# Five PSUM banks in one pool, a turned tile in the warming bank, and logits turned in 32x32 squares, in a two-layer graph attention kernel

## The chip, the cores and the metric

The kernel runs on one core of one Trainium2 chip. The time is device microseconds of one execution. The core has five engines with queues of their own: TensorE (PE in the profile; its weight loads, which overlap its products, are shown apart as PEld), VectorE (DVE), ScalarE (ACT), GpSimd (POOL) and SyncE (SP). TensorE writes its results to PSUM, a memory of eight banks, each 128 partitions by 512 f32 columns; VectorE and ScalarE empty the banks into SBUF. An engine carries out its queue in order and waits on semaphores that other engines or DMAs raise.

## The reference

512 nodes with 768 features each, 8704 edges (a random graph made symmetric, and a loop at each node). Two layers of graph attention, then a residual and a layer norm:

```
def gat_layer(x, W, a_s, a_d, b, edge_index, concat):
    h = (x @ W).reshape(n, H, C)
    alpha_s = einsum('nhc,hc->nh', h, a_s);  alpha_d = einsum('nhc,hc->nh', h, a_d)
    e = leaky_relu(alpha_s[src] + alpha_d[dst], 0.2)
    m = segment_max(e, dst);  e = exp(e - m[dst])
    alpha = e / (segment_sum(e, dst)[dst] + 1e-16)
    return segment_sum(h[src] * alpha[:, :, None], dst) + b

h   = elu(gat_layer(x, W1, a_src1, a_dst1, b1, ...))   # 8 heads of 768: W1 is 768 x 6144
out = gat_layer(h, W2, a_src2, a_dst2, b2, ...)        # 1 head: W2 is 6144 x 768
x   = layernorm(x + out)
```

## The kernel before

The edges become a dense 512x512 matrix of counts, made on the chip from the sorted edge list by products of one-hot matrices, so that each attention is a dense masked softmax and each sum over edges a matrix product. All products are f32; the profile shows an f32 product as two records. Large products use block schemes with fewer multiplications: seven products P1 to P7 of half-size blocks, or fifteen of thirds, with sums of blocks formed by VectorE or by DMAs that add. Several products add up in the same PSUM bank (`over`).

The order on each engine is that of the Python code (`manual_schedule`). It runs: load and turn x; head 0's projection x @ W1 between the counting of edges; then for each head the projection of a later head, the attention's logits and softmax, the attention product, elu, and the head's share of the second layer's projection, added up in `h2`; at last the second layer's logits, softmax and product, and the layer norm. Code for a second, general pass follows, which is entered only if the list of edges is not of the expected kind; it isn't for these inputs.

Three places are touched.

**Pools.** A tile pool in PSUM is a set of banks; a new tile takes a free bank, and its first writer waits until the bank's former tile has been read for the last time. Before, up to the end of head 0's counting stage there are `mm0` with three banks and `held` with two, the latter for product P1 of the first projection, whose bank is used again by P6, P7 and P4 (L659 to L692). Beside them stand `tr` with two banks and `bc` with one. At the end of the counting stage (`counting.close()`) `mm0` and `held` are given back, and a pool `mm` of five banks over the same space is opened for the rest.

**Turning x.** `turn_x(t, r)` (L323) turns three 128x128 squares of x by TensorE into a tile of PSUM (L327), and ScalarE copies it to `xT` (L328). After the third item of the first projection, four tiles are turned: (2, 0), (3, 0), (2, 1), (3, 1). VectorE then forms the sums `xS` (L425 to L428), of which product P5 needs the first. The pool `bc` at that time is used by nothing: at the kernel's start, products of zeros were written to it to keep TensorE's clock up (L292), which is why it is called the warming bank here. Later in the counting stage one tile of counts goes there.

**Layer 2's logits.** TensorE adds up both logits of each node in a tile `rows`, as two rows at each of the partitions 0, 32, 64 and 96 (L1535): source logits on the first, destination logits on the second. ScalarE copies it to `row2` (L1564). Then `pick`, called inside the second tile of product P7 ahead of its last piece, sums the four partial rows: one product spreads the source logits over all partitions as `BC` (L1570), and four products, one for each tile of 128 nodes, turn the destination logits into a column each of `own` (L1572):

```
nc.tensor.matmul(BC[H][:, :N], picks[:, 0:1].to_broadcast([P, P]), row2, start=True, stop=True)
for t in range(NT):
    nc.tensor.matmul(own[:, t:t + 1], row2[:, t * P:(t + 1) * P], picks[:, 1:2], start=True, stop=True)
```

VectorE copies `own` to `own2` (L1575), ScalarE adds it to `BC` tile by tile (`lift`, L723), VectorE applies the slope (L727) and takes the maximum (L732), ScalarE the exponential (L736). VectorE meanwhile subtracts or adds the products' banks to `h2` (L570) and folds a common part into it (L1530, `fold(parts[:2])` between `row2` and `pick`). Product P4 of the second layer adds to P7's banks and so waits until L570 has read them.

Other lines that the text names: L389 turns the edge indices; L383 casts them on VectorE; L445 is the product of halves; L483 to L485 empty head 1's products P1, P2 and P6; L585 sums weights on VectorE; L672 empties head 0's products on VectorE; L706 spreads logits by TensorE; L712 is a VectorE transposition of 128x32; L1033 turns the attention by DMA and L1036 puts it into `PT`; L1072 to L1075 form sums of it; L1139 and L1145 are head 0's attention products and their emptying; L1626 is the last product; L274 and L275 are sums of weights by DMA.

Of the kernel before, what the change touches and what calls it, by code (L numbers as in the profile page):

```python
# [8 lines left out]
F32 = mybir.dt.float32  # L9
# [5 lines left out]
ALU = mybir.AluOpType  # L15
AX = mybir.AxisListType
# [23 lines left out]
def gat_pass(  # L40
# [16 lines left out]
    nc = tc.nc  # L57
    P = 128
    N, D = x.shape
    H = a_src1.shape[0]  # L60
    E = src.shape[0]
    NT = N // P
# [6 lines left out]
    SQ = 32  # L69
# [4 lines left out]
    const = ctx.enter_context(tc.tile_pool(name="const", bufs=1))  # L74
# [7 lines left out]
    counting = ExitStack()  # L82
    ohp = counting.enter_context(tc.tile_pool(name="onehot", bufs=1))
    tr = ctx.enter_context(tc.tile_pool(name="tr", bufs=2, space=bass.MemoryType.PSUM))
    bc = ctx.enter_context(tc.tile_pool(name="bc", bufs=1, space=bass.MemoryType.PSUM))
    mm = counting.enter_context(tc.tile_pool(name="mm0", bufs=3, space=bass.MemoryType.PSUM))
    held = counting.enter_context(tc.tile_pool(name="held", bufs=2, space=bass.MemoryType.PSUM))

    def row_bcast(ap_row):
        return bass.AP(tensor=ap_row.tensor, offset=ap_row.offset, ap=[[0, P], [1, D]])  # L90
# [209 lines left out]
    ident = const.tile([P, P], F32, name="ident")  # L300
# [5 lines left out]
    ones = const.tile([P, 1], F32, name="ones")  # L306
    nc.vector.memset(ones, 1.0)

    picks = const.tile([P, 2], F32, name="picks")
    for j in range(2):  # L310
        nc.vector.tensor_reduce(picks[:, j:j + 1], ident.rearrange("p (j k) -> p k j", k=32)[:, j, :], axis=AX.X,
                                op=ALU.add)
    far = const.tile([P, 1], F32, name="far")
    nc.vector.memset(far, -NO_EDGE)
    tiny = const.tile([P, 1], F32, name="tiny")
# [4 lines left out]
    xT = keep.tile([P, DC, N], F32, name="xT")  # L320


    def turn_x(t, r):  # L323

        ps = mm.tile([P, 512], F32, name="mm")
        for k in range(HK):
            nc.tensor.transpose(ps[:, k * P:(k + 1) * P], x_sb[:, t, (r * HK + k) * P:(r * HK + k + 1) * P], ident)  # L327
        nc.scalar.copy(xT[:, r * HK:(r + 1) * HK, t * P:(t + 1) * P],  # L328
                       ps[:, :HALF].rearrange("p (k n) -> p k n", n=P))
# [13 lines left out]
    else:  # L343
# [5 lines left out]
        for c in range(EC):  # L349
            m = (c + 0.5) * P * N / E  # L350
            b = int(m // B)
# [96 lines left out]
    HS, AL, BC = {}, {}, {}  # L448
# [22 lines left out]
    def by_halves(hs, XA, B_, p4_apart=False):  # L471
# [19 lines left out]
        if p4_apart:  # L491
# [10 lines left out]
                 P1=("z", (0, 1), -1.0), P10=("y", (1, 1), -1.0), P5=("z", (1, 1), 1.0), P14=("x", (0, 1), -1.0),  # L502
# [149 lines left out]
    def first_projection(h, XA, B_, between):  # L652


        HS[h] = hs = hpool.tile([P, NT, D], F32, name="hs")
        new_alpha(h)
        bank = {}

        def step(p, over, i, out, op):  # L659
            def multiply():  # L660
                if over is None:
                    bank[p, i] = (held if p == "P1" else mm).tile([P, 512], F32, name="held" if p == "P1" else "mm")
                else:
                    bank[p, i] = bank[over, i]
                product(bank[p, i], XA, B_, p, i, over is None)

            def empty():
                ps, o = bank[p, i][:, :HALF], out(i)
                if op is None:
                    nc.scalar.copy(o, ps)  # L670
                else:
                    nc.vector.tensor_tensor(o, o, ps, op=op)  # L672
            return multiply, empty, op is not None

        steps = [
            ("P1", None, lambda i: hs[:, i, L], None),
            ("P2", None, lambda i: hs[:, i, L], ALU.add),
            ("P5", None, lambda i: hs[:, 2 + i, R], None),
            ("P3", "P5", lambda i: hs[:, i, R], None),
            ("P6", "P1", lambda i: hs[:, i, R], ALU.subtract),  # L680
            ("P7", "P1", lambda i: hs[:, 2 + i, R], ALU.subtract),
            ("P4", "P1", lambda i: hs[:, 2 + i, L], None),
        ]

        def firsts():
            for k in range(HK):
                if k == HK - 1:
                    between()
                for i in range(2):
                    if k == 0:  # L690
                        bank["P1", i] = held.tile([P, 512], F32, name="held")
                    nc.tensor.matmul(bank["P1", i][:, :HALF], XA["P1"][:, k, i * P:(i + 1) * P], B_["P1"][:, k, :],  # L692
                                     start=k == 0, stop=k == HK - 1, skip_group_check=True)

        items = [step(p, over, i, out, op) for p, over, out, op in steps for i in range(2)]
        for i, multiply in enumerate((firsts, lambda: None)):
            items[i] = (multiply, *items[i][1:])
        return items
# [66 lines left out]
    if not general:  # L765
# [76 lines left out]
                    done.add(t)  # L842


        turns = {3: [(2, 0), (3, 0), (2, 1), (3, 1)]}
        sums = const.tile([P, 2 * NT + 2], F32, name="sums")
        wholes = len(items)

# [13 lines left out]
        pos, made, quarter, waiting, masks = 0, set(), EC // NT, [], []  # L862
        for n, batch in enumerate(batches):
            fresh = sorted({c // quarter for c in batch} - made)
            made.update(fresh)
            if n == 0:
                waiting = [lambda k=k: destinations(k) for k in fresh]
            else:
                first = ahead_of.get(n, [])
                head = 1 if n == 1 else len(waiting)  # L870
                here = None
                if n + 1 == len(batches):
                    (k,), (before, *rest) = fresh, waiting
# [12 lines left out]
            ahead = kinds(batches[n + 1], True) if n + 1 < len(batches) else []  # L886
            items_here = max(wants[n] - pos if n < len(wants) else 0, 1)
            share = len(ahead) // (items_here + 1) if n == 0 else -(-len(ahead) // items_here)
            for f in masks:
                f()  # L890
            waiting, masks = [], []
            for f in extra.pop(n, []):
                f()
            while n < len(wants) and pos < wants[n]:
                if pos == wholes:
                    pairs = projection(1, XA, B1)
                    items += [(m, e, False) for m, e in pairs[:4]]
                multiply, empty, on_vector = items[pos]
                multiply()
                if on_vector:  # L900
                    waiting.append(empty)
                else:
                    empty()
                pos += 1
                for t, r in turns.get(pos, []):
                    turn_x(t, r)
                if pos == 1:
                    nc.scalar.activation(nidx, low, AF.Copy, bias=0.5)
                part = 0 if n == 0 and pos == 2 else share
                for c in ahead[:part]:  # L910
                    one_hot(c, True)
                del ahead[:part]
            for c in ahead:
                one_hot(c, True)
            if n == 2:
                turn_b1()
            if n == 0:
                ((k,),) = [sorted({c // quarter for c in batches[1]} - made)]
                made.add(k)
                destinations(k)  # L920
                waiting.pop()()
            uncounted += batch
            if n + 1 == len(batches):
                for t in range(NT):
                    half(t, 0)()
            if n == 2 or n + 1 == len(batches):
                count(uncounted, n > 2)
                uncounted = []
# [25 lines left out]
    else:  # L954
        for t in range(NT):
            ps = mm.tile([P, 512], F32, name="mm")
# [29 lines left out]
    counting.close()  # L986


    mm = ctx.enter_context(tc.tile_pool(name="mm", bufs=5, space=bass.MemoryType.PSUM))
    late = ctx.enter_context(tc.tile_pool(name="late", bufs=1))  # L990
    h2 = late.tile([P, NT, D], F32, name="h2")
    pass_ = late.tile([P, 2, 2 * TH], F32, name="pass")
# [7 lines left out]
    work = ctx.enter_context(tc.tile_pool(name="work", bufs=2))  # L1000
# [527 lines left out]
    def fold(parts):  # L1528
        for part, i, op in parts:
            nc.vector.tensor_tensor(part, part, u2[:, i, :], op=op)  # L1530
# [31 lines left out]
        add_rows(al2[:, :, t], ident, t, slice(t * P, (t + 1) * P), False, True)  # L1562
    row2 = work.tile([P, N], F32, name="nr")
    nc.scalar.copy(row2, rows[:, :N])  # L1564
    fold(parts[:2])
    own = tr.tile([P, 512], F32, name="tr")

    def pick():
        BC[H] = bc.tile([P, 512], F32, name="bc")
        nc.tensor.matmul(BC[H][:, :N], picks[:, 0:1].to_broadcast([P, P]), row2, start=True, stop=True)  # L1570
        for t in range(NT):
            nc.tensor.matmul(own[:, t:t + 1], row2[:, t * P:(t + 1) * P], picks[:, 1:2], start=True, stop=True)  # L1572

    pairs[7][0](pick)
    nc.vector.tensor_copy(own2, own[:, :NT])  # L1575
# [105 lines left out]
```

## Time and profile before

| | us |
|---|---|
| median of 3 executions | 615.52 (614.91 to 615.61) |
| profiled execution, its own time | 615.07 |
| its span from first to last instruction | 613.0 |
| TensorE (PE) busy | 604.9 (99%) |
| weight loads (PEld) busy | 481.9 (79%) |
| VectorE (DVE) busy | 525.3 (86%) |
| ScalarE (ACT) busy | 335.4 (55%) |
| GpSimd (POOL) busy | 145.5 (24%) |

The granted TensorE clock is 0.998 of full speed. Busy time of TensorE includes the pipeline's modelled ends, so rows of products overlap by a few hundredths to tenths of a microsecond; a row's start is the firmer number. "Idle before" is the time for which an engine stood still ahead of a row, with the instruction or DMA that ended it; idle time of an engine that nobody waits for costs nothing.

### The profile page before, as it was taken

The numbers are of one execution on the slowest core, as the hardware profiler recorded it, in microseconds if no ns is written. First come the engines' busy times: TensorE is split into PE (matmuls) and PEld (weight loads), VectorE is DVE, ScalarE is ACT, GpSimd is POOL, SyncE is SP. The second block draws the span as 40 slices with busy tenths as digits, with TensorE's granted clock in tenths as the row PEclk, the third lists the DMA queues.
The fourth block names the chain that finished last, engine by engine and source line by source line (L and its number), as shares of the span: only waits on it lengthen the run. The fifth ranks groups of instructions, "written<-read, shape, count | busy, mean of one in ns | idle before, by whom it ended". The sixth has DMA issues, their size and how long they took to land.

```text
span 613.0 us, 8592 instructions
## 1 busy us (share of the span) xinstructions
PE 604.9 (99%) x2772; PEld 481.9 (79%) x2772; DVE 525.3 (86%) x1149; ACT 335.4 (55%) x628; POOL 145.5 (24%) x182
## 2 busy tenths in 40 slices
PE   9999999999999999999999999999999999999995
PEld 5665775558888888888888888888888888885553
DVE  7999889887999879977898879977898878978785
ACT  5669776803675165823766164932757056753360
POOL 3310101032431332422431332412342303110000
PEclk9999999999999999999999999999999999999999
DMA  8992949699999998999899999999789994790032
GB/s 293 317 214 56 292 83 314 142 330 313 209 170 242 254 240 210 151 313 255 184 179 240 235 249 227 144 324 223 177 193 204 299 284 70 165 262 4 18 78 81
DMA packets 107292, 126.24 MB, mean 206 GB/s; under 512 B 41526, under 2 KB 87530, under 8 KB 106474
## 3 DMA queue, kind: packets, MB, share of 16 engines
q1 hardware_dynamic: 74813, 90.24, 48.5%
q0 software_dynamic: 32064, 35.00, 36.7%
q8 instruction: 24, 0.39, 0.3%
q10 hardware_dynamic: 365, 0.40, 0.2%
q14 instruction: 26, 0.21, 0.1%
HBM read 97.22 MB, written 2.90 MB: 163 GB/s over the span
## 4 chain that ended last, share of the span: by engine, by line
PE 97%; DVE 2%; ACT 1%; issue 0%; DVEq 0%
PE mm L527 47%; PE mm L445 19%; PE mm L1099 18%; PE mm L1139 6%; PE mm L1626 3%; PE held L445 2%; PE bc L292 1%; DVE os L804 0%; PE tr L830 0%; DVE odw L789 0%; PE tr L1535 0%; DVE here L784 0%; ACT hs L484 0%; PE tr L1020 0%; PE mm L327 0%
## 5 line engine op out<-in xcount | busy, mean ns | idle before, releaser
L533 ACT ACTIVATE hs<-mm 128x512 f32<-128x512 f32 x30 | 17.9, 596 | 83.7 <-PE mm L527 83.3
L1099 PE MATMUL mm<-PT,hs 128*128 128x256 f32 x216 | 52.5, 379 | 0.0
L736 ACT ACTIVATE q<-q,nmax 128x512 f32<-128x512 f32 x32 | 23.1, 721 | 49.0 <-DVE nmax L732 48.9
L540 DVE TENSOR_TENSOR hs<-hs,mm 128x512 f32<-128x512 f32 x45 | 30.9, 687 | 18.5 <-PE mm L527 18.1
L1099 PEld LDWEIGHTS mm<-PT,hs 128*128 128x128 f32 x216 | 41.0, 190 | 5.8
L538 POOL DMA_DIRECT2D h<-pass x22 | 26.7, 1307 | 75.9 <-ACT pass L537 75.0
L540 DVE TENSOR_TENSOR h<-h,mm 128x512 f32<-128x512 f32 x56 | 38.3, 684 | 5.8 <-PE mm L527 5.6
L1036 ACT COPY PT<-zr 128x1024 uint16<-128x1024 uint16 x34 | 39.4, 1158 | 4.8 <-DMA zr<-nr 3.2
L527 PE MATMUL mm<-w2r,xT 128*128 128x256 f32 x160 | 37.8, 379 | 0.0
L527 PE MATMUL mm<-w2r,gT 128*128 128x256 f32 x160 | 37.0, 379 | 0.0
L1099 PE MATMUL mm<-pS,gS 128*128 128x256 f32 x144 | 37.0, 379 | 0.0
L136 POOL DMA_DIRECT2D w1t<-in_L_gnn_W_dram x18 | 30.1, 1970 | 25.8 <-DVE pS L1072 25.8
L527 PE MATMUL mm<-w1t,hs 128*128 128x256 f32 x144 | 34.1, 380 | 0.0
L527 PE MATMUL mm<-w1r,hs 128*128 128x256 f32 x144 | 34.0, 379 | 0.0
L527 PE MATMUL mm<-w1r,gS 128*128 128x256 f32 x144 | 34.0, 379 | 0.0
L527 PEld LDWEIGHTS mm<-w2r,xT 128*128 128x128 f32 x160 | 30.4, 190 | 4.1
L527 PEld LDWEIGHTS mm<-w2r,gT 128*128 128x128 f32 x160 | 30.4, 190 | 4.1
L136 POOL DMA_DIRECT2D w1r<-in_L_gnn_W_dram x12 | 14.5, 1208 | 80.4 <-DMA w1r<-in_L_gnn_W_dram 45.7
L527 PEld LDWEIGHTS mm<-w1t,hs 128*128 128x128 f32 x144 | 27.3, 190 | 3.9 <-ACT absent L537 0.2
L1099 PEld LDWEIGHTS mm<-pS,gS 128*128 128x128 f32 x144 | 27.4, 190 | 3.7
L527 PEld LDWEIGHTS mm<-w1r,gS 128*128 128x128 f32 x144 | 27.3, 190 | 3.7
L527 PEld LDWEIGHTS mm<-w1r,hs 128*128 128x128 f32 x144 | 27.2, 190 | 3.8
(328 smaller groups left out, 1555.4 us busy)
## 6 DMA issues: line engine op xcount, KB each, us to landing
w2r<-in_L_gnn_W_dram SPq DMA_DIRECT2D x48, 384.0 KB
w1r<-in_L_gnn_W_dram SPq DMA_DIRECT2D x43, 384.0 KB
w1t<-in_L_gnn_W_dram SPq DMA_DIRECT2D x24, 256.0 KB
h<-pass POOLq DMA_DIRECT2D x22, 256.0 KB, 6.6
gT<-xd SPq DMA_DIRECT2D x5, 1024.0 KB
w1t<-in_L_gnn_W_dram POOLq DMA_DIRECT2D x18, 256.0 KB, 6.8
a_s<-in_L_gnn_a_src_dram SPq DMA_DIRECT2D x8, 384.0 KB
a_d<-in_L_gnn_a_dst_dram SPq DMA_DIRECT2D x8, 384.0 KB
```

Source lines behind the costliest of these rows:

```text
L136: nc.gpsimd.dma_start(o, i, accum_op=ALU.add)
L292: nc.tensor.matmul(idle[:, :cols], zeros[:, :P], zeros[:, :cols], start=True, stop=True)
L445: nc.tensor.matmul(ps[:, :HALF], A_[p][:, k, i * P:(i + 1) * P], B_[p][:, k, :], start=start and k == 0, stop=k == HK - 1, skip_group_chec ...
L527: nc.tensor.matmul(bank[chain][:, i * TH:(i + 1) * TH], A_[p][:, k, i * P:(i + 1) * P], B_[p][:, k, :], start=first and i == k == 0, stop= ...
L533: nc.scalar.activation(out(o), ps, AF.Copy, scale=sign)
L538: nc.gpsimd.dma_start(out(o), part, accum_op=ALU.add)
L540: nc.vector.tensor_tensor(out(o), out(o), ps, op=ALU.add if sign > 0 else ALU.subtract)
L736: nc.scalar.activation(q, q, AF.Exp, bias=nmax, scale=-1.0, accum_out=dens[t])
L1036: nc.scalar.copy(PT.rearrange("p s n -> p (s n)").bitcast(U16).rearrange("p (s n h) -> p s n h", s=NT, h=2)[:, :, t * P:(t + 1) * P, :], p ...
L1099: nc.tensor.matmul(bank[p][:, :HN], A_[p][:, k, c * P:(c + 1) * P], B_[p][:, k, :], start=over is None and k == 0, stop=k == 1, skip_group ...
L1139: nc.tensor.matmul(banks[c, p][:, :HN], A_[p][:, k, c * P:(c + 1) * P], B_[p][:, k, :], start=over is None and k == 0, stop=k == 1, skip_g ...
L1626: nc.tensor.matmul(ps[:, :cols.stop - cols.start], PT[:, s, t * P:(t + 1) * P], h2[:, s, cols], start=(s == 2), stop=(s == 1))
```

## The change

Three edits come together. The pool `mm` of five banks is opened at the start and lives to the end; `mm0` and `held` are gone, and so is the closing and opening between them. The turned tile (2, 1) goes to the pool `bc` instead of a bank of `mm`. For the destination logits, VectorE turns `row2` in 32x32 squares into a new tile `squares`, and four products with 32-column weights `fours` and 4-column data give `own`, each for 32 partitions; `fours` has ones where a row's and a column's place in a square agree, and takes the place of `picks`.

```
-    mm = counting.enter_context(tc.tile_pool(name="mm0", bufs=3, space=bass.MemoryType.PSUM))
-    held = counting.enter_context(tc.tile_pool(name="held", bufs=2, space=bass.MemoryType.PSUM))
+    mm = ctx.enter_context(tc.tile_pool(name="mm", bufs=5, space=bass.MemoryType.PSUM))
...
-    picks = const.tile([P, 2], F32, name="picks")
-    for j in range(2):
-        nc.vector.tensor_reduce(picks[:, j:j + 1], ident.rearrange("p (j k) -> p k j", k=32)[:, j, :], axis=AX.X,
-                                op=ALU.add)
+    fours = const.tile([P, SQ], F32, name="fours")
+    nc.vector.tensor_reduce(fours, ident.rearrange("p (j k) -> p k j", k=SQ), axis=AX.X, op=ALU.add)
...
-    def turn_x(t, r):
-
-        ps = mm.tile([P, 512], F32, name="mm")
+    def turn_x(t, r, pool=None):
+
+        ps = mm.tile([P, 512], F32, name="mm") if pool is None else pool.tile([P, 512], F32, name="bc")
         for k in range(HK):
             nc.tensor.transpose(ps[:, k * P:(k + 1) * P], x_sb[:, t, (r * HK + k) * P:(r * HK + k + 1) * P], ident)
...
-                    bank[p, i] = (held if p == "P1" else mm).tile([P, 512], F32, name="held" if p == "P1" else "mm")
+                    bank[p, i] = mm.tile([P, 512], F32, name="mm")
...
-                        bank["P1", i] = held.tile([P, 512], F32, name="held")
+                        bank["P1", i] = mm.tile([P, 512], F32, name="mm")
...
-        turns = {3: [(2, 0), (3, 0), (2, 1), (3, 1)]}
+        turns = {3: [(2, 0), (3, 0), (2, 1, bc), (3, 1)]}
...
-    mm = ctx.enter_context(tc.tile_pool(name="mm", bufs=5, space=bass.MemoryType.PSUM))
     late = ctx.enter_context(tc.tile_pool(name="late", bufs=1))
...
     row2 = work.tile([P, N], F32, name="nr")
     nc.scalar.copy(row2, rows[:, :N])
+    squares = work.tile([P, N // SQ, SQ], F32, name="nr")
+    nc.vector.transpose(squares.rearrange("p b k -> p (b k)"), row2)
     fold(parts[:2])
     own = tr.tile([P, 512], F32, name="tr")
 
     def pick():
         BC[H] = bc.tile([P, 512], F32, name="bc")
-        nc.tensor.matmul(BC[H][:, :N], picks[:, 0:1].to_broadcast([P, P]), row2, start=True, stop=True)
-        for t in range(NT):
-            nc.tensor.matmul(own[:, t:t + 1], row2[:, t * P:(t + 1) * P], picks[:, 1:2], start=True, stop=True)
+        nc.tensor.matmul(BC[H][:, :N], fours[:, 0:1].to_broadcast([P, P]), row2, start=True, stop=True)
+        for g in range(P // SQ):
+            nc.tensor.matmul(own[g * SQ:(g + 1) * SQ, :NT], fours, squares.rearrange("p (t g) k -> p g t k", t=NT)[:, g, :, 1],
+                             start=True, stop=True, tile_position=(0, g * SQ), skip_group_check=True)
```

In the changed program the order of instructions on each engine is otherwise the same; which bank a tile of `mm` has, and so what its first writer waits for, differs in the counting stage and just after it.

More of the change, by code (lines that the diff above doesn't have):

```diff
@@ L904, in gat_pass @@
                 pos += 1
-                for t, r in turns.get(pos, []):
-                    turn_x(t, r)
+                for t, r, *pool in turns.get(pos, []):
+                    turn_x(t, r, *pool)
                 if pos == 1:
```

## The prediction

> **What bounds the kernel now.** I read the page first, then the waits of TensorE's weight loads, then busy times by stage, then the timeline around each edit. The weight loads are rows named PEld. In a fence of the timeline the columns are start, duration, engine, line, operation, tiles, count and, in brackets, idle time before and what ended it. The page, with busy time by engine and the chain that ended last:
>
> ```profile
> span 613.0 us, 8592 instructions
> ...
> PE 604.9 (99%) x2772; PEld 481.9 (79%) x2772; DVE 525.3 (86%) x1149; ACT 335.4 (55%) x628; POOL 145.5 (24%) x182
> ...
> PE 97%; DVE 2%; ACT 1%; issue 0%; DVEq 0%
> ```
>
> TensorE is busy nearly always and carries 97% of the chain, so a change pays only where TensorE stands still, or where it gets fewer instructions. Where a weight load (PEld) stands idle is the finer sign; its waits for other engines, in us, times, longest:
>
> ```profile
> PEld mm L445 <- DVE h L570: 0.6, 1, 0.6
> ...
> PEld mm L445 <- ACT hs L484: 0.4, 1, 0.4
> ...
> PEld mm L327 <- DVE hs L672: 0.3, 1, 0.3
> PEld mm L445 <- DVE xS L425: 0.3, 1, 0.3
> ```
>
> All four lie at places that the change touches: the turning of x (L327, L425), the first tile from the five-bank pool (L484), the destination logits (L570). Between them stands a long stage with nothing to win (busy us by engine, clock, DMA share, GB/s):
>
> ```profile
> 141.10:559.90 418.80, 418.80 (x1934) 365.77 (x1933) 359.53 (x727) 229.41 (x418) 121.49 (x100) 1.00 0.95 218
> ```
>
> TensorE is busy 418.80 of 418.80 us there. A gain before it must be carried through it.
>
> **Part 1, a turned tile in the warming bank.** Before, the third turned tile (t=2, r=1) takes the bank of the product P2 and waits until VectorE has emptied it. The whole place:
>
> ```profile
> 9.74 0.86 ACT L328 COPY xT<-mm 128x384 f32<-128x384 f32 x2 [2.64 <-PE mm L327]
> ...
> 13.37 0.56 DVE L672 TENSOR_TENSOR hs<-hs,mm 128x384 f32<-128x384 f32 x1
> ...
> 13.62 1.79 ACT L328 COPY xT<-mm 128x384 f32<-128x384 f32 x4 [1.13 <-PE mm L327]
> ...
> 13.97 1.36 DVE L585 TENSOR_TENSOR w1t<-w1r 128x1152 f32<-128x1152 f32 x1
> ...
> 13.97 0.64 PEld L327 LDWEIGHTS mm<-ident,hs 128*128 128x128 f32 x6 [0.30 <-DVE hs L672]
> ...
> 14.69 2.10 PE L445 MATMUL mm<-w1r,xT 128*128 128x384 f32 x6
> ...
> 15.45 0.96 DVE L425 TENSOR_TENSOR xS<-xT 128x768 f32<-128x768 f32 x1
> ...
> 16.46 0.35 PEld L445 LDWEIGHTS mm<-w1t,xS 128*128 128x128 f32 x2 [0.29 <-DVE xS L425]
> ...
> 16.62 4.03 PE L445 MATMUL mm<-w1t,xS 128*128 128x384 f32 x12
> ```
>
> Now this tile goes to a free bank, and its three transpositions fill the 0.30 us. The built program's order shows that the fourth tile (t=3, r=1) now waits for that same VectorE instruction, which ends at 13.93; by then the third tile's loads (6 take 0.64, so 3 take 0.32, from 13.65) are just done, so this wait is covered to within 0.04. TensorE alone would gain 0.30. But P5 needs xS (L425), which needs the fourth copy. ScalarE copies at a pitch of 0.86 - 0.48 = 0.38; four in a row from 13.62 end at 13.62 + 3 x 0.38 + 0.48 = 15.24 instead of 13.62 + 1.79 = 15.41. L425 follows 0.04 behind, at 15.28 instead of 15.45; VectorE's L585 ahead of it, 13.97 + 1.36 = 15.33, may overlap by the few hundredths that VectorE's rows overlap elsewhere. P5 gains **0.17 us**, not 0.30. Bounds 0 and 0.30; a loss is excluded, as no work is added here.
>
> The two reductions for picks become one for fours, near 2 us; VectorE then idles 0.96 for the indices, which covers it:
>
> ```profile
> 3.24 0.89 DVE L383 CAST idx_f<-idx_i 66x256 f32<-66x256 int32 x1 [0.96 <-DMA idx_i<-in_src_dram]
> ```
>
> Without that cover it would cost a few tenths of a microsecond.
>
> **Part 2, one pool.** The old pools close after head 0, and the new five-bank pool's first bank after the spread lies over a bank that ScalarE empties at L484:
>
> ```profile
> 45.17 0.86 POOL L275 DMA_DIRECT2D w2t<-w2t  x1 [5.11 <-DMA w2t<-w2t]
> ...
> 47.91 0.35 PEld L706 LDWEIGHTS tr<-ident,wide 128*128 128x128 f32 x3 [0.18 <-issue]
> ...
> 48.10 0.48 ACT L484 COPY hs<-mm 128x384 f32<-128x384 f32 x1
> ...
> 48.63 3.52 PEld L445 LDWEIGHTS mm<-w2t,xS 128*128 128x128 f32 x12 [0.37 <-ACT hs L484]
> ```
>
> In the changed program P6 of head 1 waits for its weights' sum by DMA alone, and the next sum, which reads it, was issued at 45.17, so it had landed by then. The load moves from 48.63 to 47.91 + 0.35 = 48.26: **0.37 us**. The two L484 waits now stand before P7's second tile and P5's first, four and eight microseconds later, when the copies are long done: nothing. Bounds 0 and 0.37.
>
> Is this carried on? The near-critical place is where the turned attention comes in:
>
> ```profile
> 69.48 0.37 ACT L1145 COPY u<-mm 128x256 f32<-128x256 f32 x1 [0.38 <-PE mm L1139]
> ...
> 69.75 1.16 ACT L1036 COPY PT<-zr 128x1024 uint16<-128x1024 uint16 x1
> ...
> 70.94 0.69 DVE L1072 TENSOR_TENSOR pS<-PT 128x512 f32<-128x512 f32 x1 [1.18 <-ACT PT L1036]
> ...
> 71.67 0.69 DVE L1073 TENSOR_TENSOR pS<-pS,PT 128x512 f32<-128x512 f32 x1
> ...
> 73.38 0.84 PEld L1139 LDWEIGHTS mm<-pS,gS 128*128 128x128 f32 x4
> ```
>
> The load at 73.38 needs L1073, over at 72.36: 1.02 us of room for an advance of 0.17 + 0.37 = 0.54, and ScalarE's part ahead of it itself waited 0.38 for TensorE, so it moves along. From 141 to 560 every product follows TensorE's own releases. I carry all of 0.54.
>
> **Part 3, the squares.** Before, four one-column products (eight records, since an f32 product shows as two) each load a full 128-column weight. The end of the logits:
>
> ```profile
> 569.33 0.40 PE L1535 MATMUL tr<-ident,al 128*2 128x128 f32 x8
> ...
> 569.66 1.56 PE L445 MATMUL mm<-w2r,gT 128*128 128x384 f32 x4
> ...
> 571.05 1.02 PE L1570 MATMUL bc<-nr,picks 128*128 128x512 f32 x2
> ...
> 571.91 0.95 PE L1572 MATMUL tr<-picks,nr 128*128 128x1 f32 x8
> ...
> 572.72 0.89 PE L445 MATMUL mm<-w2r,gT 128*128 128x384 f32 x2
> ...
> 569.33 0.11 PEld L1535 LDWEIGHTS tr<-ident,al 128*2 128x2 f32 x8 [0.55 <-issue]
> ...
> 569.66 0.94 PEld L445 LDWEIGHTS mm<-w2r,gT 128*128 128x128 f32 x4 [0.22 <-issue]
> ...
> 573.57 3.52 PEld L445 LDWEIGHTS mm<-w1t,gT 128*128 128x128 f32 x12 [0.57 <-DVE h L570]
> ...
> 569.85 0.59 ACT L1564 COPY nr<-tr 128x512 f32<-128x512 f32 x1 [11.21 <-PE tr L1535]
> ...
> 569.78 1.02 DVE L1530 TENSOR_TENSOR h<-h,pass 128x384 f32<-128x384 f32 x2
> ...
> 572.90 0.16 DVE L1575 COPY own<-tr 128x4 f32<-128x4 f32 x1 [2.10 <-PE tr L1572]
> ...
> 572.98 1.23 DVE L570 TENSOR_TENSOR h<-h,mm 128x384 f32<-128x384 f32 x2
> ```
>
> The path is L1572, its copy to own at 572.90, then L570, then P4's load at 573.57, idle 0.57 until then. The new own products have 32-column weights and 4-column data. The nearest row is L1535, also in a slice of the array's columns: eight records from 569.33 to 569.66, 0.33 us, with a tail of 0.07 (0.40). Going back costs 0.10: the four records after it take 571.05 - 569.66 = 1.39, where the pitch of a record is (16.62 - 14.69) / 6 = 0.322, four of them 1.29. I charge the same 0.10 for going in. So own ends at 571.91 + 0.10 + 0.33 + 0.07 = 572.41 instead of 571.91 + 0.95 = 572.86: **0.45 us**, for VectorE's copy and P4 alike. The last piece of P7 then ends near 573.1 and does not hold P4.
>
> A rule speaks against this. The Trainium skill, "TensorEngine Tiling (Array Packing)", section Key Properties, says that a change of tiling mode drains TensorE. The trace half agrees: L1535 starts at 569.33, while the product before it still runs in the model, but its load idled 0.55. By the rule, as an estimate, own would start at the broadcast's end, 572.07, and end at 572.47, so the part would give 0.39 and the sum 0.93.
>
> VectorE's transposition is new on the path. It waits for the row, ready at 569.85 + 0.59 = 570.44; behind it stand the two L1530 sums, which used to run at 569.78, and the copy to own. Its price for 128x512 is bounded from below by another instruction of 512 columns, L1073's 0.69, and from above by sixteen times the one of 32 columns:
>
> ```profile
> 88.28 0.21 DVE L712 STREAM_TRANSPOSE turned<-wide 128x32 f32<-128x32 f32 x1
> ```
>
> That is 3.36. Most of 0.21 is a fixed part, as the 128x4 copy's 0.16 shows, so I take 0.16 + 16 x 0.05 = 0.96. Starting 0.04 after the row, the squares then end at 571.44, before 572.01 where own wants them, and L1530 ends at 571.44 - 0.08 + 1.02 = 572.38, just before 572.41. Hidden, with nothing to spare.
>
> **Sum.** 0.17 + 0.37 + 0.45 = 0.99 us. The profiled execution took 615.07 (span 613.0 and 2.1 around it), so 614.08 of its kind. The median shown is 615.52; the four executions (614.91, 615.07, 615.52, 615.61) have their middle at 615.30, which I take as the base: **614.31**, written 614.3. A measurement of this kernel can tell about 0.2%, 1.23 us, from no change; seen from 615.52 that line is 614.29, so the forecast sits on it.
>
> **Rivals.**
> - All idle goes: 0.30 + 0.37 + 0.57 = 1.24 and more if the freed TensorE pulls later waits in. 614.06, down to 613.8. For it: L585 and the copies may slip closer. Against: the copies' pitch. Chance 0.23.
> - The long stage eats Parts 1 and 2. DMA engines are 95% busy there; if one weight lands just in time, TensorE waits for it. Left is 0.45: 614.85. Against: in the whole list of waits no weight load waits for a DMA. Chance 0.12.
> - The narrow products are slow to enter: the 0.55 for which L1535's loads idled is paid in full at own, 571.91 + 0.55 + 0.40 = 572.86, as before. Part 3 gives nothing: 614.76. Against: TensorE's matmul rows show no such gap at L1535. Chance 0.08. This is the strong form of the Trainium skill's rule in "TensorEngine Tiling (Array Packing)", Key Properties.
> - Slower: VectorE's transposition is long. Up to 0.99 us it is hidden; each further microsecond delays L1530, the own copy and P4. At 2.02 it takes back the other parts' 0.54; at the bound of 3.36 the copy stands at 570.48 + 3.36 - 0.08 + 1.02 = 574.78 instead of 572.90, +1.88, net +1.34: 616.64. For it: nothing in the trace shows 512 columns. Against: the fixed part above. Chance 0.05.
>
> **How the numbers follow.** The forecast has 0.52; half of it lies on each side of the line. Faster 0.26 + 0.23 = 0.49; same 0.26 + 0.12 + 0.08 = 0.46; slower 0.05. The range takes in the first three rivals and some 0.3 of spread as among the four executions: 613.6 to 615.3.
>
> **What would show it.** In the profile after: no idle before the third tile, the xS subtraction near 15.28, head 1's P6 load near 48.09 instead of 48.63 without a ScalarE releaser, the long stage starting 0.54 earlier and just as full, the copy to own about 1.0 earlier, near 571.9, and P4's load about 1.0 earlier too, near 572.6. Wrong would be: a transposition over 1 us, an own group of TensorE longer than 0.6, P6 waiting on something new, or the long stage with holes.

## The result

| | before | changed |
|---|---|---|
| median, us | 615.61 (614.76 to 617.19, 16 executions) | 614.10 (613.60 to 615.89, 16 executions) |
| profiled execution, its span | 615.07, 613.0 | 613.75, 611.6 |

The ratio is 0.9972, 95% interval 0.9964 to 0.9981: 0.28% faster, 1.7 us (1.2 to 2.2). The two medians differ by 1.51 us. The line numbers of the changed kernel are two to four lower than those of the kernel before (L445 is now L442, L327 is L324, L425 is L422, L672 is L669, L1570 and L1572 are L1568 and L1570).

The page of the changed kernel, busy time by engine and the chain that ended last:

```profile
span 611.6 us, 8593 instructions
...
PE 603.1 (99%) x2772; PEld 480.6 (79%) x2772; DVE 525.7 (86%) x1149; ACT 334.7 (55%) x628; POOL 145.4 (24%) x182
...
PE 98%; DVE 0%; ACT 0%; issue 0%; DVEq 0%
```

The shares of VectorE and ScalarE in the chain, 2% and 1% before, are rounded to nothing now. The waits of weight loads at the places of the change:

```profile
PEld tr L1570 <- DVE h L1526: 0.8, 1, 0.8
...
PEld mm L442 <- DVE h L567: 0.5, 1, 0.5
PEld mm L442 <- DVE xS L422: 0.4, 1, 0.4
```

The two that ended on VectorE's emptying of P2 and on ScalarE's of head 1 are gone, the other two are not. One is new, of the narrow products' loads (L1570). It is the longest, but the products themselves start only 0.10 us later than full-width ones do, as wide_own below shows. The first stage in the timeline:

```profile
11.00 2.10 PE L442 MATMUL mm<-w1r,xT 128*128 128x384 f32 x6
...
13.23 0.55 DVE L669 TENSOR_TENSOR hs<-hs,mm 128x384 f32<-128x384 f32 x1
...
13.48 0.36 PEld L324 LDWEIGHTS bc<-ident,hs 128*128 128x128 f32 x3
...
13.83 0.34 PEld L324 LDWEIGHTS mm<-ident,hs 128*128 128x128 f32 x3
...
14.24 2.10 PE L442 MATMUL mm<-w1r,xT 128*128 128x384 f32 x6
...
15.12 0.96 DVE L422 TENSOR_TENSOR xS<-xT 128x768 f32<-128x768 f32 x1
...
16.13 3.52 PEld L442 LDWEIGHTS mm<-w1t,xS 128*128 128x128 f32 x12 [0.40 <-DVE xS L422]
...
16.18 4.09 PE L442 MATMUL mm<-w1t,xS 128*128 128x384 f32 x12
```

The third tile has no idle time ahead of it. P2's second tile starts 0.45 earlier (14.69 before), P5 0.44 (16.62). Of that, up to 0.16 lies ahead of the edit: the first tile of P2 stood at 11.16 before and stands at 11.00. P6 of head 0 stands at 23.98 instead of 24.36, 0.38 earlier. Head 1, after the spread of its logits:

```profile
47.53 0.36 PEld L703 LDWEIGHTS tr<-ident,wide 128*128 128x128 f32 x3 [0.18 <-issue]
...
47.73 0.48 ACT L481 COPY hs<-mm 128x384 f32<-128x384 f32 x1
...
47.86 3.53 PEld L442 LDWEIGHTS mm<-w2t,xS 128*128 128x128 f32 x12
```

P6's load follows the spread by 0.33 us instead of 0.72 and waits for nothing; it is 0.77 earlier than before (48.63). The long stage is as full as it was (window and length; busy us with instructions for PE, PEld, DVE, ACT, POOL; clock, DMA share, GB/s):

```profile
140.33:559.13 418.80, 418.80 (x1934) 365.77 (x1933) 359.52 (x727) 228.99 (x418) 121.48 (x100) 1.00 0.95 218
```

The 0.77 arrives whole at the logits, 568.56 against 569.33. Their end:

```profile
568.56 0.40 PE L1531 MATMUL tr<-ident,al 128*2 128x128 f32 x8
...
569.70 0.71 DVE L1562 STREAM_TRANSPOSE nr<-nr 128x512 f32<-128x512 f32 x1 [0.60 <-ACT nr L1560]
...
570.28 1.02 PE L1568 MATMUL bc<-nr,fours 128*128 128x512 f32 x2
570.33 0.98 DVE L1526 TENSOR_TENSOR h<-h,pass 128x384 f32<-128x384 f32 x2
...
571.24 0.24 PE L1570 MATMUL tr<-nr,fours 128*32 128x4 f32 x8
...
571.41 0.91 PE L442 MATMUL mm<-w2r,gT 128*128 128x384 f32 x2
...
571.55 0.16 DVE L1574 COPY own<-tr 128x4 f32<-128x4 f32 x1 [0.23 <-PE tr L1570]
571.63 0.55 DVE L567 TENSOR_TENSOR h<-h,mm 128x384 f32<-128x384 f32 x1
...
572.22 3.52 PEld L442 LDWEIGHTS mm<-w1t,gT 128*128 128x128 f32 x12 [0.52 <-DVE h L567]
572.23 4.14 PE L442 MATMUL mm<-w1t,gT 128*128 128x384 f32 x12
```

The own group's eight records take 571.41 - 571.24 = 0.17 us of TensorE, against 572.72 - 571.91 = 0.81 before. P4's load stands at 572.22 instead of 573.57, 1.35 earlier: 0.77 carried and 0.58 from the squares.

### The profile page after: what moved, and what is told of

Read it like the earlier page. It is cut to its first block, busy times and chain, and to the rows that moved or that the text cites. A ratio compares the mean times of both kernels' runs of the same rounds, so it can differ in the third digit from the quotient of the medians.

```text
span 611.6 us, 8593 instructions
## 1 busy us (share of the span) xinstructions
PE 603.1 (99%) x2772; PEld 480.6 (79%) x2772; DVE 525.7 (86%) x1149; ACT 334.7 (55%) x628; POOL 145.4 (24%) x182
## 4 chain that ended last, share of the span: by engine, by line
PE 98%; DVE 0%; ACT 0%; issue 0%; DVEq 0%
PE mm L524 47%; PE mm L442 22%; PE mm L1095 18%; PE mm L1135 6%; PE mm L1625 3%; PE mm L689 1%; PE bc L291 1%; PE tr L827 0%; PE mm L324 0%; PE tr L1531 0%; PE tr L1016 0%; ACT xT L325 0%; PE bc L1568 0%; DVE hs L1629 0%; PE bc L827 0%; DVE st L1631 0%
```

## The experiments

Five distances carry the comparison. Times are us from the start of the span, each from one profiled execution:

| kernel | median | ratio to before, 95% | P2's first record | P2's second tile | P5 | last spread load to P6 load, head 1 | logits' last products to the last product's first load |
|---|---|---|---|---|---|---|---|
| before | 615.61 |  | 11.16 | 14.69 | 16.62 | 0.72 | 15.72 |
| only_bank | 615.32 | 0.9999 (0.9988 to 1.0010) | 10.96 | 14.22 | 16.32 | 0.73 | 15.73 |
| only_pool | 614.70 | 0.9988 (0.9976 to 0.9999) | 10.96 | 14.54 | 16.48 | 0.33 | 15.73 |
| only_squares | 614.45 | 0.9986 (0.9975 to 0.9996) | 10.96 | 14.54 | 16.48 | 0.72 | 15.14 |
| bank_and_pool | 614.83 | 0.9994 (0.9980 to 1.0008) | 10.74 | 14.22 | 16.16 | 0.33 | 15.72 |
| changed | 614.10 | 0.9972 (0.9964 to 0.9981) | 11.00 | 14.24 | 16.18 | 0.33 | 15.14 |
| again | 613.91 | 0.9981 (0.9972 to 0.9990) | 10.57 | 14.22 | 16.16 | 0.33 | 15.13 |
| no_bank | 614.20 | 0.9982 (0.9973 to 0.9992) | 10.51 | 14.39 | 16.33 | 0.33 | 15.13 |
| early_empty | 613.64 | 0.9976 (0.9965 to 0.9986) | 11.24 | 14.48 | 16.42 | 0.33 | 14.98 |
| before_early_empty | 615.29 | 1.0001 (0.9991 to 1.0011) | 11.26 | 14.79 | 16.73 | 0.73 | 15.50 |
| three_turns | 615.05 | 0.9999 (0.9990 to 1.0008) | 11.38 | 14.62 | 16.88 | 0.33 | 16.32 |
| wide_own | 614.69 | 0.9993 (0.9984 to 1.0002) | 10.64 | 14.18 | 16.12 | 0.33 | 15.73 |
| split_sum | 613.65 | 0.9976 (0.9966 to 0.9985) | 10.76 | 14.21 | 16.14 | 0.33 | 15.15 |
| both_moves | 613.55 | 0.9974 (0.9963 to 0.9984) | 10.96 | 14.21 | 16.15 | 0.33 | 14.97 |

The kernel before, run beside them, had medians of 615.42 (beside the four kernels from only_bank to bank_and_pool), 615.13 (early_empty, before_early_empty, three_turns, wide_own) and 615.15 (again, no_bank, split_sum, both_moves).

**One part alone.** Three kernels with one edit each, and one with two, from the kernel before.

Only the bank (`turns = {3: [(2, 0), (3, 0), (2, 1, bc), (3, 1)]}`):

> The kernel before with one edit: the turned tile (2, 1) goes to the warming bank; the two pools and the picks stay. Theory (the parts add up, each by its own mechanism): no idle before the third turned tile, the first xS sum some 0.2 us earlier against the first product of P2, P5 earlier by as much, and the whole 0.2 us faster (0.03%). Rival (the gain of the three parts hangs on the pools, so one alone gives nothing, because head 1's P6 still waits at its old place for ScalarE): the sum xS is earlier, but by head 1's P6 nothing is left, time as before. Rival (part of the 1.4 us between the two traces is the landing of x at the start, which differs from execution to execution): the first product of P1 stands anywhere between 6.35 and 6.55 us, whichever edits are in.

No gain that can be told. In its trace P2's second tile does start 0.32 us earlier than in only_squares, which had the same start and the old bank (14.22 against 14.54), but little is left of it at P6, and the xS sum is no earlier than there. Here VectorE waited for a weight:

```profile
14.04 1.36 DVE L585 TENSOR_TENSOR w1t<-w1r 128x1152 f32<-128x1152 f32 x1 [0.26 <-DMA w1r<-in_L_gnn_W_dram]
...
15.32 0.95 DVE L425 TENSOR_TENSOR xS<-xT 128x768 f32<-128x768 f32 x1
...
16.32 4.14 PE L445 MATMUL mm<-w1t,xS 128*128 128x384 f32 x12
...
24.17 4.03 PE L445 MATMUL held<-w1t,xS 128*128 128x384 f32 x12
```

So a third releaser, the landing of w1r, can take the gain: at 24.17 it stands only 0.05 ahead of only_squares (24.22). The first rival's "nothing is left" nearly came true in this execution, but not for its cause: the gain was lost at P5, where the load idled 0.61 us, and the 0.05 left at P6 of head 0 still stands as 0.04 at P6 of head 1 (48.44 against 48.48). With the old pools and an earlier weight the bank alone was not seen.

Only the pool (`mm` of five banks from the start, `mm0` and `held` gone):

> The kernel before with one edit: one pool of five banks from the first stage to the last; the third turned tile stays in that pool, and the picks stay. Theory: head 1's P6 load follows the spread of the logits at once, without waiting for ScalarE's emptying, which is worth 0.37 to 0.39 us there, and the long stage carries it: 0.4 us faster in all (0.06%). The idle of 0.30 us before the third turned tile may stay, move or change, as the tile takes another bank. Rival (that wait is replaced by one on the weights' sum by DMA): the load stands at its old place against the spread, with a DMA as releaser, and the time is as before.

The load of P6 follows the spread by 0.33 instead of 0.72, with no releaser, as expected: 0.39 us, and the idle before the third tile is still there (0.36).

Only the squares:

> The kernel before with one edit: the destination logits are turned in squares by VectorE, with fours for picks; pools and turned tile as before. Theory: all as before up to the logits; then the group of own takes 0.2 to 0.3 us of TensorE instead of 0.8, own is copied some 0.55 us earlier and P4 loads 0.55 to 0.6 earlier, and the time is 0.58 us shorter (0.09%). Rival (the gain after the logits in the trace of the changed kernel came from its earlier stages, which gave VectorE another order of arrival): 0.45 or less.

From the logits' last products to the last product's first load it takes 15.14 instead of 15.72: 0.58 us, with nothing else changed.

Bank and pool without the squares:

> The changed kernel without the squares: pool and turned tile changed, picks and the four full-width products of own as before. Theory: 0.2 + 0.4 = 0.6 us faster than before (0.10%), arriving whole at the logits; P4's load at the end as late after the last P7 product as before. If the start of the kernel differs by chance, the distance between the first product of P2 and the load of head 1's P6 is still 0.6 shorter than before. Rival (the two overlap, since both shift the same waits of the counting stage): 0.4.

The interval of the ratio holds theory, rival and no gain at all. The trace has both parts: 14.22 as with the bank alone, 0.33 as with the pool alone, and 15.72 at the end as before. Its P6 load of head 1, at 47.76, is 0.72 earlier than that of only_squares (48.48): 0.32 and 0.39. The parts add up. The distance named beforehand, from P2's first record to that load, missed: it is 37.02 against 37.47 before, 0.45 shorter and not 0.6, since an early start of P2, as here (10.74), is not kept; the experiments with the bank below say why.

**What the squares saved.** The own products kept their four columns of data from the squares, but got full-width weights, so that own no longer holds the logits:

```
-            nc.tensor.matmul(own[g * SQ:(g + 1) * SQ, :NT], fours, squares.rearrange(...)[:, g, :, 1],
-                             start=True, stop=True, tile_position=(0, g * SQ), skip_group_check=True)
+            nc.tensor.matmul(own[:, :NT], fours[:, 0:1].to_broadcast([P, P]), squares.rearrange(...)[:, g, :, 1],
+                             start=True, stop=True)
```

> The changed kernel with the four own products given full 128-column weights (fours' first column spread over all), on all partitions and outside the narrow tiles; the data are the squares' four columns as before. The values in own are not the logits. It tells what made the own group short: weights of 32 columns, or products of 4 columns in number and length. Theory (the load of a weight sets the pitch of so short a product): eight records at 0.10 us as in the kernel before, 0.81 us in place of 0.17, no entry of 0.10 ahead of it, and copy, P4 and end 0.5 to 0.6 us later than in the changed kernel. Rival (a short product costs 0.02 to 0.04 whatever its weights): as the changed kernel, less the entry, 0.1 us earlier.

All of the 0.58 is gone (15.73). The rows of wide_own:

```profile
570.31 1.02 PE L1568 MATMUL bc<-nr,fours 128*128 128x512 f32 x2
...
571.17 0.95 PE L1570 MATMUL tr<-nr,fours 128*128 128x4 f32 x8
...
571.98 0.89 PE L442 MATMUL mm<-w2r,gT 128*128 128x384 f32 x2
...
572.16 0.16 DVE L1574 COPY own<-tr 128x4 f32<-128x4 f32 x1 [0.81 <-PE tr L1570]
```

Eight records take 0.81 us again, 0.10 each, with 128 columns of weights, and 0.17, 0.021 each, with 32. The data were the same, so the width of the weights sets the pitch, or the quarter of the array's columns that each narrow product has to itself: this run changes both and does not part them. Own stands 571.17 - 570.31 = 0.86 behind the broadcast here and 571.24 - 570.28 = 0.96 in the changed kernel: the entry into narrow products costs 0.10. The Trainium skill, "TensorE: Matmul & The Clock Gate", section LDWEIGHTS (loading the stationary operand), gives the time of a weight load as its columns divided by 1.2 in ns; as an estimate from it, eight loads are 0.85 us at 128 columns and 0.21 at 32. The traces' 0.81 and 0.17 agree, 5% and 20% below.

**Time of TensorE, or the wait for own?** One VectorE instruction is moved: the first tile of P7 is emptied before the transposition, so that P4 need not wait behind the copy to own. First in the changed kernel, then in the kernel before:

```
-        pairs[6][0])
+        pairs[6][0], pairs[6][1])
...
-    run(pairs[6][1], pairs[7][1], pairs[8][0], pairs[9][0])
+    run(pairs[7][1], pairs[8][0], pairs[9][0])
```

> The changed kernel with one VectorE instruction moved: the first tile of P7 is added to h2 (L567) right after its product, ahead of the transposition, in the 0.60 us for which VectorE waits there, and no longer behind the copy to own. Theory (in the changed kernel P4's load still stands behind own, by 0.52 us, since L567 is queued behind the copy): P4 loads 0.50 us earlier, at the pitch of TensorE's records, own comes at its old time, and the end is 0.5 us earlier (0.08%). Rival (the softmax that hangs on own sets the end as soon as P4 is free): P4 earlier, the last product's chain less than 0.2 us earlier.

> The same move in the kernel before: the first tile of P7 is added to h2 right after its product and not behind the copy to own. It tells which half of own's price the squares took away, TensorE's own time or the wait for the copy. Theory (TensorE's time alone: the own group cost 0.81 us of TensorE's records and now 0.27, which is nearly the whole gain of 0.58, and the wait of 0.52 to 0.57 behind it is another one that the squares left as it was): P4's load 0.52 to 0.55 us earlier than in the kernel before, and so nearly level, within 0.1 us, with the changed kernel's when both are counted from the start of the logits' last products. Rival (the gain of the squares was the wait for own): with the wait gone there is 0.2 us or less between this kernel and the squares with the early emptying.

Both were off in size. Counted from the logits' last products, P4's load comes 0.37 us earlier in the changed kernel, not 0.50, and the end only 15.14 - 14.98 = 0.16. In the kernel before the load comes 0.44 earlier, not 0.52 to 0.55, which leaves it 0.14 behind the changed kernel's and not within 0.1, and the end 15.72 - 15.50 = 0.22. The squares are worth 15.50 - 14.98 = 0.52 without the wait and 0.58 with it, so the rival of the second kernel falls: what they saved is TensorE's own time. Why 0.52 us of idle load are worth 0.16 shows in early_empty:

```profile
571.66 0.91 PE L442 MATMUL mm<-w2r,gT 128*128 128x384 f32 x2
...
572.09 3.74 PEld L442 LDWEIGHTS mm<-w1t,gT 128*128 128x128 f32 x12
...
572.41 4.03 PE L442 MATMUL mm<-w1t,gT 128*128 128x384 f32 x12
```

With its weight on time, P4's first record stands 572.41 - 571.66 = 0.75 behind P7's last two; in the changed kernel, with 0.52 us of idle load, 572.23 - 571.41 = 0.82. The records before it stream on while the load waits. Lost are 0.07 at the first record and, as the twelve records take 4.14 instead of 4.03, about 0.1 before the loads are a record ahead again. The 0.16 is whole at the next twelve records (576.28 - 568.80 = 7.48 behind the logits' last products, 576.20 - 568.56 = 7.64 in the changed kernel), before the softmax has a say: the first kernel's rival had the number but not the cause.

The transposition done three times over (`for _ in range(3):` around it):

> The changed kernel with the transposition done three times over into the same tile: VectorE has 3 x 0.71 = 2.13 us of it in place of 0.71, near the 2.02 us at which the prediction's slower rival had the parts 1 and 2 taken back. Theory (the chain is row, transpositions, then own and the fold side by side, then the copy): the squares end 1.42 later, TensorE stands still 0.6 us ahead of own, the fold ends 1.42 later and the copy to own with it, at 1.2 us later than in the changed kernel (it had 0.23 us of idle VectorE ahead of it), P4 and the end 1.2 later: some 1.2 us slower than the changed kernel, level with the kernel before to within 0.3 us. Rival (own waits for nothing on VectorE but the first transposition, or P4 finds other cover): 0.6 us or less.

The theory holds. The copy to own stands 4.17 behind the logits' last products instead of 2.99, and the end comes 16.32 - 15.14 = 1.18 later. VectorE's row of three is 2.20 - 0.71 = 1.49 us longer, not the 1.42 expected. Against the kernel before the time is level.

```profile
569.79 0.40 PE L1531 MATMUL tr<-ident,al 128*2 128x128 f32 x8
...
570.93 2.20 DVE L1563 STREAM_TRANSPOSE nr<-nr 128x512 f32<-128x512 f32 x3 [0.60 <-ACT nr L1560]
...
573.05 0.98 DVE L1526 TENSOR_TENSOR h<-h,pass 128x384 f32<-128x384 f32 x2
...
573.19 0.25 PE L1571 MATMUL tr<-nr,fours 128*32 128x4 f32 x8 [0.65 <-DVE nr L1563]
...
573.96 0.15 DVE L1575 COPY own<-tr 128x4 f32<-128x4 f32 x1
```

So 1.49 - 1.18 = 0.31 us of cover were left: as an estimate from this, a transposition up to 0.71 + 0.31 = 1.02 us is hidden. What was beyond the cover came through whole, 1.18 at the copy and 1.18 at the end.

**What the bank is worth, and what holds P5.** The changed kernel again; the same without the bank; with the first xS sum in halves; and with this and the early emptying together:

```
+        def s1():
+            for i in range(2):
+                a, b = slice(i * P, (i + 1) * P), slice(HN + i * P, HN + (i + 1) * P)
+                nc.vector.tensor_tensor(xS[:, 0, :, a], xT[:, :HK, b], xT[:, HK:, b], op=ALU.subtract)
```

> The changed kernel once more, beside the three that follow, for its time on the same chip and for a second look at its start. Theory: the landing of the first weights and of x differs from execution to execution, so that P2's first record stands anywhere from 10.6 to 11.4 us, and this spread, not an edit, is the 0.16 us by which the two first traces already differ there; from L1531, the logits' last products, to the last product's first load it is 15.14 us again, within 0.03. Rival (the edits make the start shorter): P2's first record at 11.00 within 0.05.

> The changed kernel with the turned tile (2, 1) back in the five-bank pool: one pool and squares without the warming bank. Theory (the idle of 0.30 us before short transpositions is TensorE's own time in full, and P5 is not held by xS, since its first record stands one pitch of 0.322 behind P2's last in both traces): the load of the third turned tile idles 0.30 to 0.36, P5's first record stands 0.25 to 0.30 later than in the changed kernel, at 16.45 to 16.6 us, and the whole is as much slower. Rival (the prediction's step: ScalarE's copies and the xS sum set P5): 0.17 us or less.

> The changed kernel with the first xS sum (L422) made in two halves, one for each tile of P5, so that P5's first load need not wait for the second half: the load's idle of 0.40 us should go. Theory (idle time of a weight load ahead of a 384-column product is mostly hidden behind the two records before it): P5's first record moves from 16.18 by 0.02 us or less, P6 and the rest by 0.05 to 0.10 us, since only the refilling of the loads ahead is saved; the time is the same. Rival (the idle of the load row is TensorE's loss): 0.40 us faster, P6 at 23.6 us.

> The changed kernel with both moves: the first xS sum in two halves, and the first tile of P7 emptied ahead of the transposition. Theory (from the early emptying's trace: 0.16 us at the last product for 0.52 us of the load's idle; 0.05 to 0.10 us from the halves): 0.2 us faster than the changed kernel. Rival (the two idle times of the load rows, 0.40 and 0.52): 0.9 us faster.

The start: P2's first record stands at 10.51 to 11.38 in the fourteen traces, and not by edits (before 11.16, only_squares with the same first stage 10.96; changed 11.00, again 10.57). That part of the difference is chance. But little of an early start is kept, since a turned tile waits for VectorE's emptying of P2, which started at 13.20 to 13.24 in nine of the fourteen, however early P2 was. In these nine P2 began at 11.00 or earlier, and VectorE was still busy with the counting (L786 in the changed kernel) ahead of the emptying. Where P2 began at 11.16 or later (four traces), the emptying started 2.20 to 2.21 us behind it. From again:

```profile
10.57 2.10 PE L442 MATMUL mm<-w1r,xT 128*128 128x384 f32 x6
...
12.02 1.29 DVE L786 TENSOR_TENSOR odw<-here,weight 128x2176 bf16<-128x2176 bf16 x1
...
13.23 0.55 DVE L669 TENSOR_TENSOR hs<-hs,mm 128x384 f32<-128x384 f32 x1
...
13.83 0.31 PEld L324 LDWEIGHTS mm<-ident,hs 128*128 128x128 f32 x3 [0.42 <-DVE hs L669]
...
14.22 2.10 PE L442 MATMUL mm<-w1r,xT 128*128 128x384 f32 x6
...
16.16 4.03 PE L442 MATMUL mm<-w1t,xS 128*128 128x384 f32 x12
```

Without the bank the third and the fourth tile wait there, and the three transpositions between, 0.32 us, come behind: 14.54 in only_pool and only_squares. Counted from the start of the emptying, which takes the differing starts out, P2's second tile stands 1.31 to 1.32 behind it in all five traces without the bank and 0.98 to 1.04 in all nine with it. So the bank is worth about 0.3 us there. no_bank itself missed its numbers: the load idled 0.66, not 0.30 to 0.36, and P5 stood at 16.33, 0.17 behind again. Its rows say why that is not the rival's 0.17:

```profile
13.08 0.55 DVE L669 TENSOR_TENSOR hs<-hs,mm 128x384 f32<-128x384 f32 x1
...
13.68 0.64 PEld L324 LDWEIGHTS mm<-ident,hs 128*128 128x128 f32 x6 [0.66 <-DVE hs L669]
...
14.39 2.10 PE L442 MATMUL mm<-w1r,xT 128*128 128x384 f32 x6
...
16.33 4.03 PE L442 MATMUL mm<-w1t,xS 128*128 128x384 f32 x12
```

VectorE was 0.15 us earlier in this execution (13.08), as it was all through its counting from 4.62 on (4.77 in again), ahead of any edit. P5 stands 16.33 - 14.39 = 1.94 behind P2's second tile, as in again (16.16 - 14.22): TensorE's pitch, not xS, sets it here. In only_bank and three_turns, where VectorE waited 0.26 and 0.46 us for w1r, xS came too late for that: the load at P5 idled 0.61 and 0.77 us, and P6 stood 9.95 and 10.10 behind P2's second tile, where it stands 9.67 to 9.75 behind in the other twelve traces. split_sum bears out the first. The load at P5 no longer idles in split_sum, and P5 stands at 16.14 instead of 16.16, P6 at 23.88 instead of 23.90. Against the first trace of the changed kernel, whose load came at 16.13, just ahead of the record, it gains 0.06 more, as the twelve records take 4.03 instead of 4.09.

both_moves is the fastest: 613.55 us, beside 613.91 for the changed kernel on the same chip. The intervals of the ratios overlap; the trace has 14.97 against 15.13 at the end, 0.16 us, all from the early emptying. No rival's 0.9 us was there.

## Why the prediction was right, and where its steps failed

The time came out 0.2 us below the forecast, inside the range. The gain was undersized: forecast 0.99, measured 1.51 between the medians, and 0.99 lies below the interval of 1.2 to 2.2. The time is nearer than the gain because the base was taken 0.31 us too low, which is luck. The traces below account for 1.21 us; the medians of again and of the kernel beside it differ by 1.24.

- **What bounds it: right.** TensorE carries the chain before and after, and the long stage neither eats nor adds: 0.77 at its entry, 0.77 at 568.56. The rival that it eats parts 1 and 2 falls with that.
- **Part 1: near in size, wrong in mechanism.** The step that failed is "P5 gains 0.17 us, not 0.30", with ScalarE's copies and the xS sum as what P5 waits for. The copies and xS went as forecast: xS stood at 15.12 and not 15.28, by the 0.16 that the first stage was early. But in both traces P5 starts one tile's pitch behind P2's second tile (16.62 - 14.69 = 1.93; 16.18 - 14.24 = 1.94): the load's idle ahead of it, 0.29 before and 0.40 now, delays no record. So the 0.30 came through: 0.28 between the two traces at P5 (0.44 less 0.16 of start), 0.30 against only_squares with nearly the same start (16.18 against 16.48), less 0.06 over P5 in the changed kernel, whose twelve records took 4.09. That leaves 0.24 at P6, where other pairs have 0.05 (only_bank against only_squares), 0.17 (again against no_bank) and 0.37 (bank_and_pool against only_pool): nearness to 0.17 depends on the pair of executions. What caps the gain is VectorE's L669; xS held P5 only in only_bank and three_turns, where w1r landed late. The prediction let the third tile's loads start at 13.65, where the row before them ends at 13.10 + 0.58 = 13.68; that changes nothing. That the fourth tile's wait is "covered to within 0.04" held in the first trace and not in again, where the start was earlier and that load idled 0.42. The reduction for fours took 0.37 us against 0.23 for picks, and VectorE still idled 0.99 for the indices behind it, so it was covered as forecast.
- **Part 2: right.** Forecast 0.37, which was also the upper bound; measured 0.39 to 0.40 (0.72 or 0.73 to 0.33), in three pairs of kernels.
- **Part 3: the term mis-sized is the own group's records**, 0.33 us after L1535's row, measured 0.17. L1535 has 128 columns of data, own only four. The entry of 0.10 was right. The path over the copy and L570 to P4 is the order in which P4 is released, but worth only 0.16 to 0.22 by itself (early_empty, before_early_empty); the copy, less the 0.77 carried in, came 0.13 earlier than forecast, and the part gave 0.58 instead of 0.45. The transposition took 0.71, at the lower bound of 0.69, not 0.96: the sixteen stretches of 32 columns cost 0.034 each, not 0.05. "Hidden up to 0.99" was near: 1.02 by three_turns.
- **The sum.** Between the traces it is 0.38 at P6 of head 0, 0.39 and 0.58, together 1.35, as at P4. Of the 0.38, 0.14 is a late start of the profiled execution of the kernel before (P5 at 16.62, against 16.48 in only_pool and only_squares, which also lack the bank) and 0.24 is part 1, so that the edits gave 1.21 us there.
- **The base** of 615.30 was 0.3 below the median of 16 executions (615.61), and within what the other medians of that kernel show (615.13 to 615.42).
- **The rivals.** "All idle goes", 1.24 us, came nearest in its sum, but not for its reason: 0.52 and 0.40 us of load idle are still there and cost 0.16 and 0.06 at most, while part 3's gain is records. The rival of the slow entry falls: 0.10, not 0.55. The Trainium skill's rule on drains ("TensorEngine Tiling (Array Packing)", Key Properties) would have put own at the broadcast's end in the trace, 570.28 + 1.02 = 571.30; it stood at 571.24. Since that end is modelled, the 0.06 do not decide on the rule; the entry cost 0.10 here. The slower rival's mechanism is real, as three_turns shows, and its price was not met.

## What to carry to other kernels

Price a wait on TensorE by the starts of the product records on both sides, not by the idle time of the weight load: where 384-column records still streamed, 0.3 to 0.6 us of idle load cost 0 to 0.27 us here, and 0.77 cost 0.42; behind short 128-column transpositions 0.30 cost 0.28 and 0.37 cost 0.39. For products with hardly any data, count weight columns: 32 instead of 128, each product in a quarter of the array's columns, made eight records 0.17 us instead of 0.81. An edit that frees an early stage is worth what the next releaser leaves of it, and that releaser (VectorE's queue, TensorE or a landing weight) differed between executions of the same stage.

## What the runs showed of the hardware

- A VectorE transposition of 128x512 f32 in 32x32 squares took 0.71 us, where 128x32 took 0.21 and a two-input sum of 512 columns 0.69: by these, 0.18 of the small one's price does not grow with its length (estimate: 0.50 us for 480 columns more), and the long one costs about as much as the sum of its length. Three in a row took 2.20.
- After a weight load that came late, twelve 384-column records took 4.14 us instead of 4.03, in the kernel before at P6 and P4 and in the changed one at P4: about 0.1 us was lost until loads were a record ahead again.
- The pitch of a four-column record was 0.021 us with 32 columns of weights, in a quarter of the array each, and 0.10 with 128. The 32-column loads idled 0.76 us ahead of the first, and their products started 0.10 us later behind the same broadcast than those of 128 columns.
